# Edges of a four-stage graph network in two groups by source: rows of the last five blocks by one-hot products

## The chip, the core and the metric

The kernel runs on one core of one Trainium2 chip. The metric is the device time in microseconds of one execution; the smaller, the better. The engines are named as in the profile: PE (matrix products), PEld (PE's loads of the stationary operand, which overlap its products), DVE (VectorE), ACT (ScalarE), POOL (GpSimd) and SP (here only an issuer of DMAs).

## What is computed

There are 3125 nodes with 128 features and 53125 directed edges, sorted by destination, one of them a loop of each node. Four graph networks run one after the other, each followed by a residual sum and a layer normalisation:

```python
x = layernorm(x + gin(x))          # 4 layers: h = x + sum over edges of x[src]; x = relu(h@W1+b1)@W2+b2
x = layernorm(x + rgcn(x))         # relu(x@root + bias + sum_r mean_{edges of type r}(x[src]) @ W[r]), 8 types
x = layernorm(x + basis(x))        # relu(sum over edges of alpha[t]*x[src]@w_rel[t] + indegree * x@update), 16 types, 8 bases
x = layernorm(x + gated(x))        # relu(sum over edges of gate*(x[src]@W[r] + bias[r]) + x@loop), 8 types
# in gated: gate = sigmoid(dot(msg, gate_weight[r]) + gate_bias[r]), so it depends on the source node and r alone
# in basis: alpha = sigmoid(h@w2), h of the edge features, but taken by edge type (alphas[rels]): 16 rows count
```

## The kernel before

**The dense stage.** The four layers of the first network use one matrix, the number of edges from each source to each destination. It lies in SBUF as `AT`, bf16, 25 blocks of 128 sources by 3125 destinations. It is built from 416 tiles of 128 edges (the loop at L796 to L842): DVE makes two one-hot matrices of a tile, `ohs` of the source inside its block (L824) and `ohk` of source block and relative destination together (L826), PE multiplies them (L828, and L832 for the column shared with the tile before), and ACT writes the product to `AT` at a place held in a register (L835). Beside this loop, at the tiles listed in `LATE`, `late` turns the edges' keys (`turn`, four PE transposes and a copy each) into the layout with one edge per partition and stores them in DRAM as `keys` and `srcs`. The dense products of the first layer are woven into the loop (`under`). Then the layers run in seven chunks of up to 512 destinations each: `dense` multiplies 25 source blocks, each as three bf16 parts, with `AT` (75 products, L760), copies the sum out on DVE as `hT` (L765), applies the two weight matrices, and stores three bf16 parts of the result. The last layer's `norm` stores its rows to the DRAM table `fx0`.

**The relational stages.** The other three networks share `relational` (L1092). It goes over the 416 tiles in order of destination. For each tile POOL gathers the 128 source rows from a DRAM table (`gather`, L1062); DVE makes a one-hot matrix `oh` of 16 destinations by 8 relations (or bases), weighted in layers 2 and 3 (L1150, L1152, L1157); PE multiplies rows and one-hot in fp32 (L1159); and DVE adds the 128x128 product to `sums` at a column held in a register (L1161). `sums` holds, for each of the 128 features, node by relation. In layers 1 and 3 small products (L1167) count a tile's edges by destination and relation into one or two segments of 128 nodes; where they go comes from two registers per tile (`seg`, loaded on PE by `values`). Before a block of `sums` is used ACT clears it (L957).

When the last tile that can touch a block of 128 nodes is through, `finish` closes the block: eight products with the relations' weights (`by_relation`, L1183), the residual and the norm, and a store. In layer 1 the sums are first divided by the counts: `sel` products spread the reciprocal counts over all partitions (L1204), and DVE multiplies (L1205). The next layer gathers from the whole table that these stores make: `fx1` for layer 2, `gtab` (rows and eight gates) for layer 3. Between layers 1 and 2 sixteen edges' end rows are gathered (`f_xs`, `f_xd`) for the attention coefficients.

**What orders the work.** Each engine runs its own instructions in the order in which a scheduler placed them; engines wait for one another by semaphores. How far POOL's gathers may run ahead of PE is set by the pool `f_gat`: six buffers of four tiles. The product L1159 has three PSUM buffers.

Of the kernel before, what the change touches and what calls it, by code (L numbers as in the profile page):

```python
# [23 lines left out]
I32 = mybir.dt.int32  # L24
# [37 lines left out]
LATE = [16, 20, 24, 28, 32, 36]  # L62
# [452 lines left out]
def gin_layers(ctx: ExitStack, tc: tile.TileContext, a: dict, pre: dict, outer: ExitStack, eps, srcI, xtab):  # L515
# [13 lines left out]
    keys = dram.tile([P, 4, TE], F32, name="keys")  # L529
    srcs = dram.tile([P, TE], I32, name="srcs")  # L530

    AT = big.tile([P, NB, N + W], BF16, name="AT")
    places = keep_.tile([P, 2, TE], F32, name="places")
# [5 lines left out]
    lo, hi = pre["lo"], pre["hi"]  # L539
# [6 lines left out]
    for n, (name, pad) in enumerate((("dst", PADDST), ("src", 0), ("edge_type_8", 0), ("edge_type_16", 0))):  # L546
        eng = (nc.sync, nc.scalar)[n % 2]
        r = raw[name] = tmp.tile([QR, 4, P], I32, name="raw_" + name)
        nc.gpsimd.memset(r[96:QR], pad)
        e = a[name]  # L550
        flat = r.rearrange("q k p -> q (k p)")

        for q0, q1 in ((0, 96), (96, QR - 1)):
            eng.dma_start(flat[q0:q1, :], e[q0 * 4 * P:q1 * 4 * P].rearrange("(q p) -> q p", q=q1 - q0))
        eng.dma_start(flat[QR - 1:QR, :E - (QR - 1) * 4 * P], e[(QR - 1) * 4 * P:].rearrange("(q p) -> q p", q=1))
    early = keep_.tile([P, 1], F32, name="early")
    nc.scalar.copy(early, eps)
    make_identity(nc, ident)
    nc.gpsimd.iota(iotah, pattern=[[1, NK]], base=0, channel_multiplier=0, allow_small_or_imprecise_dtypes=True)
    nc.gpsimd.iota(iota, pattern=[[1, 2 * P]], base=0, channel_multiplier=0, allow_small_or_imprecise_dtypes=True)  # L560
# [11 lines left out]
    def fl(name, into=None):  # L572
        f[name] = into if into is not None else tmp.tile([QR, 4, P], F32, name="f_" + name)
# [14 lines left out]
    sbI = tmp.tile([QR, 4, P], I32, name="sbI")  # L588
    nc.vector.tensor_scalar(sbI, raw["src"], 7, None, op0=OP.arith_shift_right)
    sb = tmp.tile([QR, 4, P], F32, name="sb")  # L590
    nc.vector.tensor_copy(sb, sbI)
    kb = tmp.tile([QR, 4, P], F32, name="kb")
    nc.vector.scalar_tensor_tensor(kb, sb, float(WK), rel, op0=OP.mult, op1=OP.add)
    mod = tmp.tile([QR, 4, P], F32, name="mod")
# [17 lines left out]
    nc.scalar.copy(hi, dst0[:, 1, :])  # L612
# [11 lines left out]
    def later(i, r):  # L624
        t = tmp.tile([P, TE], F32, name="turned", bufs=2)
        turn(t, r, nc.scalar.copy)
        nc.sync.dma_start(keys[:, i, :], t)

    turnedI = tmp.tile([P, TE], I32, name="turnedI")

    def late(i):

        if i == 0:
            turn(turnedI, f["src"], nc.vector.tensor_copy)
            nc.sync.dma_start(srcs[:, :], turnedI)
        elif i == 1:
            later(0, rel)
        elif i == 2:
            t8 = fl("edge_type_8", sb)
            later(3, t8)  # L640
        elif i == 3:
            nc.vector.scalar_tensor_tensor(mod, rel, float(R8), f["edge_type_8"], op0=OP.mult, op1=OP.add)
            later(1, mod)
        elif i == 4:
            later(2, fl("edge_type_16", kb))
        elif i == 5:
            flat = f["dst"].rearrange("q k p -> q (k p)")
            inner = f["src"].rearrange("q k p -> q (k p)")[:, :4 * P - 1]
            nc.vector.tensor_tensor(inner, flat[:, :4 * P - 1], flat[:, 1:], OP.is_gt)
            nc.vector.tensor_reduce(found, inner, AX.X, OP.add)  # L650
            tmp_ctx.close()

    def checks(own):
# [25 lines left out]
        add(1, w[:, 0:1], float(N - W), OP.is_lt)  # L679
        rows = own.tile([1, 1], F32, name="rows")  # L680
# [122 lines left out]
    with tc.tile_pool(name="g_hot", bufs=4) as hots:  # L803
        old = None
        under = []
        for t in range(TE):
# [6 lines left out]
            if t == LATE[-1]:  # L813
# [5 lines left out]
                nc.scalar.dma_start(srcI, srcs[:, :])  # L819
                sp_pool = sp_ctx.enter_context(tc.tile_pool(name="g_parts", bufs=1, side="right"))  # L820
            if t % 4 == 1 and (t - LATE[-1]) // 4 - 1 in range(NCH):
                first_parts((t - LATE[-1]) // 4 - 1)
# [22 lines left out]
    keep_ctx.close()  # L845
    ep = outer.enter_context(tc.tile_pool(name="f_edges", bufs=1))
    edges = ep.tile([P, 4, TE], F32, name="edges")
    nc.scalar.dma_start(edges, keys[:, :, :])
# [38 lines left out]
    for j in range(NCH):  # L887
        run(dense(l, j, norm))
    sp_ctx.close()
# [16 lines left out]

def low(t):
# [10 lines left out]
def first_tile(c0):  # L918

    return min(t for t in range(TE) if low(t)[1] + W > c0)  # L920
# [3 lines left out]
def in_order(ctx: ExitStack, tc: tile.TileContext, a: dict, out: bass.AP, pre: dict):  # L924
# [7 lines left out]
    ident, iota, ones, lo = (pre[k] for k in ("ident", "iota", "ones", "lo"))  # L932
# [7 lines left out]
    srcI = own.tile([P, TE], I32, name="f_srcI")  # L940
    edges = gin_layers(tc, a, pre, ctx, eps, srcI, xtab[0])
    dlr, key8, et16, et8 = (edges[:, i, :] for i in range(4))

    big = ctx.enter_context(tc.tile_pool(name="f_sums", bufs=1, side="right"))
    gat = ctx.enter_context(tc.tile_pool(name="f_gat", bufs=6, side="right"))
    ohp = ctx.enter_context(tc.tile_pool(name="f_ohp", bufs=6, side="right"))
# [6 lines left out]
    zero = const.tile([P, 1], F32, name="f_zero")  # L953
    nc.vector.memset(zero, 0.0)

    def clear(b, engine=nc.scalar.copy):
        engine(sums[:, b * P * NR:(b + 1) * P * NR], zero.to_broadcast([P, P * NR]))  # L957

    clear(0, nc.vector.tensor_copy)


    offs = const.tile([1, TE], I32, name="f_offs")
    nc.vector.tensor_scalar(offs, lo, float(NR), None, op0=OP.mult)
    seg = const.tile([1, 2, TE], I32, name="f_seg")

    def segments(t):
        c = low(t)
        return range(c[0] // SEGN, min(NSEG - 1, (c[1] + W - 1) // SEGN) + 1)

    def spots(t, i):  # L970

        if len(segments(t)) <= i:
            return 0, SEGN + W
# [369 lines left out]
```

## Time and profile before

| | us |
|---|---|
| Runs of the kernel, median of 3 | 2834.49 |
| lowest and highest | 2826.18, 2836.43 |
| The profiled execution's own time | 2817.4 |
| its span in the trace | 2815.5 |

| Engine | busy us | share of the span |
|---|---|---|
| PE | 1940.1 | 69% |
| PEld | 1373.8 | 49% |
| DVE | 1164.4 | 41% |
| ACT | 497.1 | 18% |
| POOL | 1191.8 | 42% |

The mean granted clock of PE over the execution is 0.698 of full speed. A busy PE is not a PE at its peak[...]. Loads of registers, waits and DMA issues are not counted as busy. A line number in the profile is that of the listing above. A group of instructions is shown as line, engine, operation and operands (output, then inputs), with the number of instructions; an fp32 product appears as two records. What a wait is put down to is the event that came last: "issue" means that the engine waited for nothing the profile shows, and "remote" that the releaser is unknown to it.

### The profile page before, as it was taken

The numbers are of one execution on the slowest core, as the hardware profiler recorded it, in microseconds if no ns is written. First come the engines' busy times: TensorE is split into PE (matmuls) and PEld (weight loads), VectorE is DVE, ScalarE is ACT, GpSimd is POOL, SyncE is SP. The second block draws the span as 40 slices with busy tenths as digits, with TensorE's granted clock in tenths as the row PEclk, the third lists the DMA queues.
The fourth block names the chain that finished last, engine by engine and source line by source line (L and its number), as shares of the span: only waits on it lengthen the run. The fifth ranks groups of instructions, "written<-read, shape, count | busy, mean of one in ns | idle before, by whom it ended". The sixth has DMA issues, their size and how long they took to land.

```text
span 2815.5 us, 37365 instructions
## 1 busy us (share of the span) xinstructions
PE 1940.1 (69%) x10916; PEld 1373.8 (49%) x10916; DVE 1164.4 (41%) x4732; ACT 497.1 (18%) x1001; POOL 1191.8 (42%) x1263
## 2 busy tenths in 40 slices
PE   5798999998467777777545656665644666565666
PEld 2343444444355566566444545554433555454545
DVE  6777612123144444444433434443423343333443
ACT  5778511101200000000001222222220000000000
POOL 0000000000545555656546666666625555555552
PEclk9988899999555655656666666666665556566666
DMA  1000111021211111111111112111211222121121
GB/s 49 17 7 13 41 46 59 19 62 46 54 47 44 44 44 45 48 43 49 45 34 50 51 50 51 49 51 49 53 28 43 48 46 47 45 49 45 45 49 26
DMA packets 101232, 121.96 MB, mean 43 GB/s; under 512 B 25046, under 2 KB 80523, under 8 KB 101031
## 3 DMA queue, kind: packets, MB, share of 16 engines
q0 software_dynamic: 40000, 83.59, 12.3%
q1 hardware_dynamic: 50256, 28.48, 3.4%
q10 hardware_dynamic: 10774, 7.42, 0.9%
q8 instruction: 100, 1.64, 0.3%
q14 instruction: 102, 0.83, 0.1%
HBM read 104.55 MB, written 14.84 MB: 42 GB/s over the span
## 4 chain that ended last, share of the span: by engine, by line
PE 47%; another core or an unknown queue 17%; issue 15%; POOL 8%; DVE 7%; DMA 3%; ACT 2%; DVEq 0%; ACTq 0%; SPq 0%; POOLq 0%
PE acc L760 14%; PE pw L1159 12%; POOL xg L1062 8%; PE pm L1183 7%; PE pa L828 3%; PE pr L1204 3%; PE pc L1167 2%; DVE sums L1161 2%; PE pr L768 1%; PE pr L775 1%; ACT AT L835 1%; DMA xn<-in_x_dram 1%; PE pa L832 1%; DMA xg<-fx,f_srcI 1%
## 5 line engine op out<-in xcount | busy, mean ns | idle before, releaser
L1062 POOL DMA_INDIRECT xg<-fx,f_srcI x832 | 791.8, 952 | 1209.5 <-DMA f_gloop<-n_L_gnn_loop_weight_dram 703.8
L1159 PE MATMUL pw<-oh,xg 128*128 128x128 f32 x2496 | 669.2, 407 | 379.9 <-DVE sums L1161 155.0
L1159 PEld LDWEIGHTS pw<-oh,xg 128*128 128x128 f32 x2496 | 524.5, 283 | 471.1 <-DVE sums L1161 188.1
L1161 DVE TENSOR_TENSOR sums<-pw,sums 128x128 f32 x1248 | 358.6, 287 | 877.0 <-remote 428.6
L1062 POOL DMA_INDIRECT xg<-gtab,f_srcI x416 | 394.5, 948 | 341.4 <-PE pw L1159 171.3
L760 PE MATMUL acc<-AT,xs 128*128 128x512 bf16 (+1 forms) x2100 | 446.2, 357 | 1.1 <-DMA xs<-xsd 1.0
L760 PEld LDWEIGHTS <-xs 128*128 128x128 bf16 x2100 | 176.3, 100 | 197.0 <-issue 22.6
L835 ACT CAST AT<-pa 128x400 f32 x416 | 213.0, 512 | 65.5 <-PE pa L832 33.3
L828 PE MATMUL pa<-ohk,ohs 128*128 128x425 bf16 x416 | 170.2, 423 | 50.1 <-ACT AT L835 25.9
L826 DVE TENSOR_SCALAR ohk<-iotah,places 128x425 bf16<-128x425 f16 x416 | 139.1, 334 | 62.2 <-PE pa L832 56.2
L957 ACT COPY sums<-f_zero 128x1024 f32<-128x1024 f32 x74 | 75.2, 1042 | 378.2 <-PE pm L1183 160.7
L1152 DVE SCALAR_TENSOR_TENSOR oh<-f_dcol,edges,coef 128x128 f32<-128x128 f32 x416 | 137.0, 343 | 0.6 <-ACT coef L1109 0.6
L1157 DVE TENSOR_SCALAR oh<-p_iota,edges,g 128x128 f32<-128x128 f32 x416 | 135.5, 354 | 0.1
L1167 PE MATMUL pc<-hw,h 128*8 128x16 f32 x1456 | 85.3, 186 | 60.8 <-issue 56.1
L1150 DVE TENSOR_SCALAR oh<-p_iota,edges 128x128 f32<-128x128 f32 x416 | 119.1, 293 | 0.0
L1183 PE MATMUL pm<-f_gW,sums 128*128 128x128 f32 x400 | 100.5, 433 | 25.0 <-DVE sums L1161 18.6
L1204 PE MATMUL pr<-ci,f_sel 8*128 8x128 f32 x400 | 93.4, 379 | 31.5 <-DVE sc L1205 22.2
L1167 PE MATMUL pc<-hw,rg 128*8 128x16 f32 x1456 | 83.8, 182 | 39.9 <-issue 24.3
L1183 PEld LDWEIGHTS pm<-f_gW,sums 128*128 128x128 f32 x400 | 97.9, 336 | 26.3 <-DVE sums L1161 19.4
L1167 PEld LDWEIGHTS pc<-hw,h 128*8 128x8 f32 x1456 | 61.3, 90 | 98.4 <-issue 85.8
L1183 PE MATMUL pm<-f_bases,sums 128*128 128x128 f32 x400 | 100.9, 434 | 9.1 <-issue 7.8
L828 PEld LDWEIGHTS <-ohs 128*128 128x128 bf16 x416 | 42.5, 102 | 129.9 <-DVE ohk L826 85.7
(202 smaller groups left out, 1777.9 us busy)
## 6 DMA issues: line engine op xcount, KB each, us to landing
xg<-fx,f_srcI POOLq DMA_INDIRECT x832
xsd<-sp SPq DMA_DIRECT2D x18, 384.0 KB
xg<-gtab,f_srcI POOLq DMA_INDIRECT x416
xs<-xsd SPq DMA_DIRECT2D x9, 384.0 KB
xs<-xsd ACTq DMA_DIRECT2D x9, 384.0 KB
xb<-fx SPq DMA_DIRECT2D x49, 64.0 KB
gtab<-yg SPq DMA_DIRECT2D x25, 68.0 KB
fx<-y SPq DMA_DIRECT2D x25, 64.0 KB
```

The source lines that it names most:

```text
L760: nc.tensor.matmul(acc[:, :n], xs[s // BPB][:, s % BPB, i, :], AT[:, s, c0:c1], start=s == 0 and i == 0, stop=s == NB - 1 and i == 2)
L826: nc.vector.tensor_scalar(ohk, iotah, keyb[:, t:t + 1], None, op0=OP.is_equal)
L828: nc.tensor.matmul(ps, ohs, ohk, start=True, stop=t == 0)
L835: nc.scalar.copy(AT[:, :, bass.ds(og[t % GRP], W)], ps3[:, :, :W])
L1062: nc.gpsimd.indirect_dma_start(out=dst, out_offset=None, in_=table, in_offset=bass.IndirectOffsetOnAxis(ap=idx, axis=0))
L1152: nc.vector.scalar_tensor_tensor(oh.rearrange("p (d b) -> p d b", b=NR), W2["dcol"], dlr[:, u:u + 1], cgroups[u - u % GRP][:, u % GRP, :]. ...
L1157: nc.vector.tensor_scalar(oh, iota[:, :W * NR], key8[:, u:u + 1], gate, op0=OP.is_equal, op1=OP.mult)
L1159: nc.tensor.matmul(ps, x[:, u % 4, :D], oh, start=True, stop=True)
L1161: nc.vector.tensor_tensor(w, ps, w, OP.add)
L1167: nc.tensor.matmul(segs[j][:, bass.ds(spot[i][u], W)], r, hw[:, u % GRP, :], start=False, stop=u == last_tile(min(N, (j + 1) * P)))
L1183: nc.tensor.matmul(pb, s[:, r, :], w[:, r, :], start=False, stop=r == NR - 1)
L1204: nc.tensor.matmul(pr[:, r * P:(r + 1) * P], sel[:, h + r, :], ci, start=True, stop=True)
```

## The change

The edges are split into two groups by source. Group P holds those whose source is in the last five blocks of nodes (`KB = 5`, from node `S0 = 2560` on), in 80 tiles; group G the others, in 344 tiles. Inside a group the order by destination is kept.

- **Placing the edges.** `late` computes the rank of each edge in its group on 125 partitions of 425 edges (a scan and a product with a triangular matrix) and so its slot. `scatter` writes source, destination and types of 125 edges, 8 bytes each, to their slots in DRAM: 425 indirect DMAs on POOL, one with each tile of the build loop from the 30th on and the remaining 38 behind the loop. `arrange`, called after the third chunk of the last dense layer, reads the slots back and unpacks them on DVE, with two copies held where they stand in program order. The turning of four keys in `late` goes.
- **Rows of group P** are not gathered. The last five blocks of the table stay in SBUF as three bf16 parts (`parts`, made by `keep_parts` when such a block is finished). `fetch` takes a tile's source numbers, spread over all partitions by a DMA on SP (one for two tiles), compares them with five columns of node numbers on DVE, and multiplies: 15 bf16 products into `px`, copied out by ACT. `add_P` then makes a one-hot matrix of 62 destinations by 8 relations, one product of 496 columns into `pp`, adds the old first column group on DVE, and ACT overwrites the sums from there on; so nothing is cleared any more. `px` and `pp` have one PSUM buffer each.
- **Group G** goes as before through `gather`, from the first 2560 rows of the table alone, with five gather buffers instead of six and one PSUM tile of four parts. The calls of `fetch` and `add_P` are placed between its tiles (`upto`).
- **Counts:** one register per tile on PE (`loP`) and segments with a margin of 128, instead of two registers; layer 1 counts in bf16. For group P, whole windows are counted into `cntP`.
- **Layer 1's finish** multiplies first and divides afterwards: the counts are transposed, and eight operations on DVE each scale a relation's product and add it. The `sel` products, the bias product and L1205 go.
- The keys of the tiles (`regs`, `dlr`, `key8`) are worked out before layer 1 from the unpacked edges, on DVE, most of them on one row of 424 values.

The core of the diff:

```diff
+KB = 5
+S0 = (NB - KB) * P
+NTP = 80
+NTG = 344
+WP = 62
...
     def late(i):
...
+            nc.vector.tensor_tensor_scan(rank, flag2, none, 0.0, OP.add, OP.add)
...
+    def scatter(c):
+        st = nc.gpsimd.indirect_dma_start(
+            out=slots[:, :], out_offset=bass.IndirectOffsetOnAxis(ap=rowI[:, c:c + 1], axis=0),
+            in_=meta[:EP2, c, :], in_offset=None)
...
+            if t > LATE[-1]:
+                scatter(t - LATE[-1] - 1)
...
+    def arrange():
+        def last_in_line(x):
+            tc.keep_in_program_order(x)
+        held = meta[:, :NTT, :]
+        nc.gpsimd.dma_start(held.rearrange("p t f -> p (t f)"), slots.rearrange("(p t) f -> p (t f)", p=P))
+        last_in_line(nc.vector.tensor_copy(edges["dst"], held[:, :, 0]))
...
     for j in range(NCH):
         run(dense(l, j, norm))
+        if j == 2:
+            arrange()
...
-    gat = ctx.enter_context(tc.tile_pool(name="f_gat", bufs=6, side="right"))
-    ohp = ctx.enter_context(tc.tile_pool(name="f_ohp", bufs=6, side="right"))
+    gat = ctx.enter_context(tc.tile_pool(name="f_gat", bufs=5, side="right"))
+    ohp = ctx.enter_context(tc.tile_pool(name="f_ohp", bufs=4, side="right"))
...
+        def fetch(v):
+            if v % 2 == 0:
+                srcb = wk.tile([P, 2 * P], F16, name="srcb", bufs=4)
+                nc.sync.dma_start(srcb, flatrow[:, v * P:(v + 2) * P].to_broadcast([P, 2 * P]))
+                ohT = hot_src[0] = wk.tile([P, KB, 2 * P], BF16, name="ohTP")
+                for k in range(KB):
+                    nc.vector.tensor_scalar(ohT[:, k, :], srcb, colid[:, k:k + 1], None, op0=OP.is_equal)
+            if v % 4 == 0:
+                fetched[v // 4] = (wk.tile([P, 4, GX], F32, name="xP"),)
+            ohT, x = hot_src[0], fetched[v // 4][0]
+            px = psum.tile([P, GX], F32, name="px", bufs=1)
+            for k in range(KB):
+                for i in range(3):
+                    nc.tensor.matmul(px[:, :width_], ohT[:, k, v % 2 * P:(v % 2 + 1) * P], parts[layer][:, k, i, :width_],
+                                     start=k == 0 and i == 0, stop=k == KB - 1 and i == 2)
+            nc.scalar.copy(x[:, v % 4, :width_], px[:, :width_])
+
+        def add_P(v):
...
+            oh = onehot(v, gate)
+            ps = psum.tile([P, BANK], F32, name="pp", bufs=1)
+            nc.tensor.matmul(ps[:, :WP * NR], x[:, v % 4, :D], oh, start=True, stop=True)
+            if counted:
+                pq = psum.tile([P, P], F32, name="pm", bufs=2)[:R8, :WP]
+                nc.tensor.matmul(pq, r, g["hw"][:, q, :], start=True, stop=True)
+            if v > 0:
+                nc.vector.tensor_tensor(ps[:, :NR], ps[:, :NR], sums3[:, bass.ds(g["lo"][q], 1), :].rearrange("p d r -> p (d r)"), OP.add)
...
+            nc.scalar.copy(sums3[:, bass.ds(g["loA"][q], WP), :], ps[:, :WP * NR].rearrange("p (d r) -> p d r", r=NR))
...
+        for u in range(NTG):
...
+            gather(xg[:, u % 4, :width_], table, srcI[:, w:w + 1])
+            upto(last_of(range(NTP), min(N, low2(w)[1] + W)), True)
...
     def finish1(b, s, pc):
...
+        nc.tensor.transpose(pt[:, :R8], cntP[:, blk], ident[:R8, :R8])
...
             for r in range(BPB):
-                nc.tensor.matmul(pr[:, r * P:(r + 1) * P], sel[:, h + r, :], ci, start=True, stop=True)
-            nc.vector.tensor_tensor(sc[:, h:h + BPB, :], s[:, h:h + BPB, :], pr.rearrange("p (r d) -> p r d", d=P), OP.mult)
+                nc.tensor.matmul(pr[:, r * D:(r + 1) * D], s[:, h + r, :], rW[:, h + r, :], start=True, stop=True)
+            for r in range(BPB):
+                v = wk.tile([P, D], F32, name="acc")
+                nc.vector.scalar_tensor_tensor(v, pr[:, r * D:(r + 1) * D], ci[:, h + r:h + r + 1], acc, op0=OP.mult, op1=OP.add)
+                acc = v
...
-    relational(1, xtab[0][:N, :], D, finish1, beside1)
+    relational(1, xtab[0][:S0, :], D, finish1, beside1)
...
-    relational(2, xtab[1][:, :], D, finish2)
+    relational(2, xtab[1][:S0, :], D, finish2)
...
-    relational(3, gtab[:, :], GX, finish3)
+    relational(3, gtab[:S0, :], GX, finish3)
```

## The prediction

> **What bounds the kernel now.** I cut the span by stage first, because a mean over five unlike stages says little. The cuts come from the first instruction of each stage in the trace: the build of the adjacency starts at 97 us, the dense layers alone at 330, the relational layers 1, 2 and 3 at 708, 1434 and 2083. The columns are window, length, busy time of PE, PE's weight loads, VectorE (DVE), ScalarE (ACT) and GpSimd (POOL), then PE's granted clock, DMA share, GB/s.
>
> ```profile
> 97.00:330.00 233.00, 213.14 (x1108) 92.93 (x1107) 177.56 (x725) 181.26 (x355) 0.00 (x0) 0.85 0.03 10
> 330.00:708.00 378.00, 363.69 (x1953) 172.21 (x1951) 89.12 (x271) 47.90 (x77) 0.00 (x0) 0.98 0.17 51
> 708.00:1434.00 726.00, 500.43 (x3222) 408.27 (x3222) 309.53 (x1195) 57.55 (x115) 396.67 (x418) 0.60 0.17 44
> 1434.00:2083.00 649.00, 382.74 (x1603) 320.62 (x1603) 254.45 (x1063) 137.31 (x281) 396.88 (x417) 0.63 0.19 48
> 2083.00:2815.00 732.00, 428.49 (x2832) 359.55 (x2832) 273.86 (x1265) 20.54 (x76) 394.50 (x416) 0.62 0.20 45
> ```
>
> The two dense stages are PE's own (91 and 96% busy) and POOL does nothing in them. The three relational layers take 2107 us of 2815.5, and there no engine is full: PE 69, 59 and 59%, POOL 54 to 61%, and the clock is at 0.60 to 0.63. So I read next what the gathers wait for, and the start of a layer.
>
> ```profile
> L1062 POOL DMA_INDIRECT xg<-fx,f_srcI x832: 938/944/1626, 708.2 to 2041.0; - x167
> ...
>   PE pw L1159: 345.7, 104
>   issue: 329.7, 1068
> ```
> ```profile
> 708.17 1.10 POOL L1062 DMA_INDIRECT xg<-fx,f_srcI  x1 [703.75 <-DMA f_gloop<-n_L_gnn_loop_weight_dram]
> 709.58 0.94 POOL L1062 DMA_INDIRECT xg<-fx,f_srcI  x1 [0.31 <-issue]
> 710.83 0.94 POOL L1062 DMA_INDIRECT xg<-fx,f_srcI  x1 [0.30 <-issue]
> ```
> ```profile
> 708.00:735.00 27.00, 7.61 (x61) 5.40 (x62) 1.79 (x8) 5.42 (x6) 20.43 (x22) 0.50 0.23 60
> 1434.00:1462.00 28.00, 11.93 (x42) 8.19 (x42) 6.52 (x26) 1.73 (x7) 21.30 (x23) 0.50 0.19 49
> 2083.00:2110.00 27.00, 5.60 (x32) 4.41 (x32) 3.84 (x16) 0.17 (x2) 18.67 (x20) 0.50 0.23 52
> ```
>
> One gather is 0.94 us and 0.30 of issue, so 1.247 us apart: 416 of them are a floor of 519 us a layer, under 649 to 732. But 345.7 us of POOL's idleness end at the product L1159, which frees a buffer. So POOL is ahead of PE by its 24 buffers, and PE, with gaps, carries the rest. The last table shows where gaps are widest: at each layer's start POOL issues 20 to 23 gathers in a row and PE is busy only 5.6 to 11.9 us of 27.
>
> What fills the gaps elsewhere is read from the waits of the sums and from PE's queue:
>
> ```profile
>   remote: 428.6, 114
>   PE pw L1159: 317.6, 204
> ```
> ```profile
> L1056 PEldq TENSOR_LOAD <-f_seg x206: 329/591/1717, 700.4 to 2792.4; - x103
> L1056 DVEq TENSOR_LOAD <-f_offs x78: 1095/1098/1360, 702.8 to 2786.7; - x78
> ```
> ```profile
> 721.63 0.21 PE L1167 MATMUL pc<-hw,h 128*8 128x16 f32 x2 [1.32 <-issue]
> 723.76 0.18 PE L1167 MATMUL pc<-hw,h 128*8 128x16 f32 x1 [1.92 <-issue]
> 724.47 0.19 PE L1167 MATMUL pc<-hw,h 128*8 128x16 f32 x1 [0.53 <-issue]
> ```
>
> The first fence (idle before L1161, by what ended it): the trace names no owner for 428.6 us. The second: PE loads registers 206 times at 0.59 us. The third lies inside the first layer's start: small products stand 0.7 to 2.1 us apart and wait for nothing that is recorded, while POOL issues without a break. I have no cause for this; I use it only as a fact.
>
> **The change, part by part.** Sums are against the profiled run (2817.4 us, span 2815.5), which lies 17 us under the median of 2834.5.
>
> *Gathers.* 344 instead of 416 a layer: floor 344 x 1.247 = 429 us, 90 less. As POOL waits for PE, this is worth nothing by itself; it is worth what PE can use.
>
> *PE, removed.* 72 fewer products L1159 at 0.536 us (669.2 us over 1248 tiles): 39 us a layer. In layer 1 the `sel` products L1204 (93 us) and the bias products L1210 (18 us) go. Counting products fall from 728 to 596 a layer (85 us a layer before, 0.117 each), and layer 1 counts in bf16, where I take half: layer 1 saves 50, layer 3 15. Register loads fall from 103 to 43 a layer, 35 us in each of layers 1 and 3, which is queue time and not in the busy figures.
>
> *PE, added.* Fetch: 15 bf16 products of 128 columns for each of 80 tiles, 1200 a layer. No row has this shape. The nearest is the bf16 weight load of L760, also 128 columns (the groups by line: 176.3 us over 2100, 100 ns), and each fetch product needs one: 120 us. The Trainium skill, "TensorE: Matmul & The Clock Gate", section "Back-to-back issue gap", gives about 81 ns sustained for pairs of this width: 97 us, 23 less a layer, 69 in all. I keep the row; at the clock of 0.62 the same load would be 160 ns and 193 us. Wide products L1375: fp32, 496 columns, two records each as for L768 (128x512, 0.644 us a record): 1.29 x 80 = 103 us. So PE's work at these prices is: layer 1 500 - 39 - 111 - 50 + 223 + 10 (transposes of the counts) = 533; layer 2 383 - 39 + 223 = 567; layer 3 428 - 39 - 15 + 223 = 597.
>
> *The clock.* PE was granted 0.60 to 0.63 at 59 to 69% busy and 0.85 to 0.98 at 91 to 96% in the same trace. The added bf16 products are work that waits for no gather and stands singly between the gathered tiles, so PE should be fuller and faster. I take 50 to 55 us a layer off the old fp32 work (334 us in layer 2: 184 gathered, 100 L1183, 50 rest, by a sixth): 483, 512, 542. Without a gain in clock these 160 us are lost.
>
> *From work to time.* Before, PE filled 59 to 69%; the dense stages reach 91 to 96%. I take 80% between, since register loads, PSUM buffers of one (`px`, `pp`) and the unnamed gaps stay: 483/0.80 + 25 (43 loads at 0.59) = 629; 512/0.80 = 640; 542/0.80 + 25 = 703. Against 726, 649, 732: -97, -9, -29, together -135. The shorter layer starts are in this: gathers of a layer read only the first 20 blocks, so they start while the last five are finished. Only PE's idle time there can be saved, at 1400 to 1462 us 26 and at 2040 to 2110 us 35.
>
> *DVE and ACT* gain 80 wide one-hots, 200 compares and 80 adds on DVE and 160 copies on ACT a layer. A 128x512 fp32 operation is 0.69 us on DVE (L716) and L835's 128x400 0.51 us on ACT: +140 and +90 us less what goes (L1205, L957, 72 tiles at 0.6), so DVE near 375, 330 and 360 of 630 to 700. PE hides it; without that cover the chain product, add, copy of one P tile (about 2.2 us, one `pp`) would cost 80 x 2.2 = 176 us a layer. SP's 40 broadcasts of source rows have four buffers and stand among stores that are not waited for.
>
> *The new front.* Some 20 DVE operations of 125x425 at 0.58 us (12 us) replace four turns on PE and ACT beside the build. In the build DVE is 76% busy, so I take +5. Then 425 scatters, POOL's, from build tile 29 (115 us) at the gathers' 1.247: 530 us, done at 645. They are needed by `arrange`, held on DVE after the third chunk of the last layer; the next `hT` copy, queued behind it, was at 651.7. Reading the slots back and copying them (about 5 us) just fits: +5. Before layer 1, about 30 operations on one row of 424 (0.579 each for 1x416, L607) and the split of the last blocks stand on DVE between the last norm and the first sum, 712.8 before: 25 us, of which the 19 us of PE's idleness in the first 27 were lost anyway: +5, since gathers are there by then. I round these three to +10.
>
> Here a rule speaks against the change. By the rows, 137 gathers that ran under 0.6 us or more of a DVE one-hot lasted as long (median 944 ns) as the rest, so a scatter under the build should cost the same. The Trainium skill, "SBUF — State Buffer", section "SBUF: two separate sides", says that DVE in its fast two-port modes locks GpSimd out, so that a DMA's descriptors cannot be written. The build's one-hots are fast ones: (334 - 248)/(425 - 128) = 0.29 ns a column. If scatters moved only in DVE's free 24% until 330, about 41 of 172 would be done, 131 late by 163 us, and `arrange` would hold DVE, and then PE, some 150 us: 2840 rather than 2690. I take the row, with this as an upper bound. The lower bound is zero, since a wait cannot shorten the build.
>
> Sum: 2817.4 - 135 + 10 = 2692; against the median 2834.5 - 125 = 2710.
>
> **The rivals.**
>
> *PE becomes the bound and stays gappy* (0.22). For: 223 us of new work a layer, and the gaps without an owner are in PE's completions. Against: fill products without a DMA behind them. At the old 59 to 69%, say 70%: 715, 731, 799, together +138: 2835 + 148 = 2983. It decides from a filling of 74% down.
>
> *POOL's stream slows the dense layers* (0.22). Slower, one mechanism: POOL, silent under GIN before, now issues a DMA each 1.25 us from 115 to 645, the density at which PE got 28% (7.6 of 27) in the fence of the layer starts. For: that fence, three times. Against: there PE also waited for data, and a scatter moves 1 KB, a gather 64. Slowed by a fifth over 530 us: +106 and the gain is nearly gone; by 40%, +212, 2920. It decides from 24%. The late scatters above (+150) go with it.
>
> *Nothing moves* (0.06): both halves cancel within 14 us. That the split does nothing is excluded: 72 gathers a layer are gone from POOL's queue.
>
> **How the numbers follow.** My case has 0.50: 2710, from 2495 (filling 90%: layers 562, 569, 627) to 2815. About 0.5%, 14 us, is what can be told from no change here. Faster 0.50, same 0.06, slower 0.44. The range must reach into both slower cases: 2500 to 3040.
>
> **What would show it.** Layer lengths near 630, 640, 700 with PE near 80% and a clock over 0.7; gathers 344 a layer; no PE gap of 10 us or more at the layer boundaries. Wrong: dense chunks at more than 18.4 us under the scatters; a long wait of DVE at the unpacking, about 650 us; fetch products over 0.16 us; a clock still at 0.62; idle time at `px` or `pp`.

## The result: slower, and the profile after

The changed kernel takes 2989.93 us (median of 4; 2976.85 to 2999.73) beside 2831.64 for the kernel before: ratio 1.0557, 95% interval 1.0517 to 1.0596. The profiled execution's span is 2997.6 us. I forecast 2710.

First the stages, cut at 114 us inside the build, at the build's end, at the last dense chunk (835.9 us, 694.2 before) and at the end of each relational layer. Columns as in the tables before. (The build's first product stands at 22.0 us here and at 13.5 before; the 97 us that the prediction calls its start is about where the first dense products are woven in.)

```profile
114.00:453.00 339.00, 234.03 (x1039) 78.36 (x1050) 200.94 (x700) 175.34 (x343) 270.17 (x227) 0.82 0.11 8
453.00:836.50 383.50, 363.96 (x1897) 172.44 (x1930) 82.62 (x207) 34.86 (x61) 183.93 (x158) 0.98 0.20 44
836.50:1583.30 746.80, 566.79 (x3274) 408.25 (x3274) 393.23 (x1760) 96.34 (x307) 349.79 (x364) 0.70 0.18 45
1583.30:2262.60 679.30, 527.47 (x2882) 400.79 (x2882) 346.83 (x1338) 178.44 (x428) 333.81 (x346) 0.76 0.18 44
2262.60:2997.50 734.90, 573.57 (x3872) 421.43 (x3871) 349.37 (x1563) 96.39 (x293) 307.90 (x324) 0.76 0.18 39
```

All of the loss has two places. The last dense chunk ends 142 us later: the first chunk is 20 late (140.5 against 120.9), the build loses another 103 (its last tile at 451.7 against 328.6), and 19 come behind it, at the borders of the dense layers (their short last chunk takes 11.8 and 11.5 us in the first two, 4.5 and 4.6 before); each full chunk of the dense layers still takes 18.4 us. The relational part takes 2162 us instead of 2121, where I expected about 1990: PE has gaps of 22 to 24%, not far from the 20% I assumed, but more work in between.

What runs under the build, from the group tables for 120 to 440 us after, and 97 to 330 us before (POOL, ACT and DVE; the last columns are the idle time ahead and what ended it):

```profile
L705 POOL DMA_INDIRECT slots<-meta,rowI x214 | 255.1, 1192 | 65.2 <-issue 65.2
L899 ACT CAST AT<-pa 128x400 f32 x306 | 156.5, 511 | 153.3 <-PE pa L896 134.1 <-issue 5.5 <-remote 4.0
L890 DVE TENSOR_SCALAR ohk<-iotah,places 128x425 bf16<-128x425 f16 x305 | 112.9, 370 | 121.8 <-PE pa L896 110.7 <-issue 5.7 <-remote 1.6
L888 DVE TENSOR_SCALAR ohs<-iotah,places 128x128 bf16<-128x128 f16 x305 | 98.5, 323 | 0.0
```
```profile
L835 ACT CAST AT<-pa 128x400 f32 x340 | 174.0, 512 | 50.0 <-PE pa L832 29.5 <-ACT AT L835 1.0
L826 DVE TENSOR_SCALAR ohk<-iotah,places 128x425 bf16<-128x425 f16 x338 | 113.3, 335 | 50.5 <-PE pa L832 46.2
L824 DVE TENSOR_SCALAR ohs<-iotah,places 128x128 bf16<-128x128 f16 x337 | 83.5, 248 | 0.0
```

ACT's casts last as long as before, but wait 134 us for PE instead of 30. DVE's one-hots, beside the scatters, are 35 and 75 ns longer. A scatter is 1.18 us plus 0.30 of issue, 1.485 apart, not the gathers' 1.247.

In the relational layers the page's groups show this:

```profile
L1428 PE MATMUL pw<-oh,xg 128*128 128x128 f32 x2064 | 611.9, 389 | 262.5 <-DVE sums L1430 193.7
L1361 PE MATMUL px<-f_parts,ohTP 128*128 128x128 bf16 (+1 forms) x3600 | 374.9, 248 | 58.6 <-ACT xP L1363 39.7
L1375 PE MATMUL pp<-ohP,xP 128*128 128x496 f32 x480 | 304.9, 722 | 26.1 <-ACT sums L1384 20.4
```

The new products cost what was priced. But the product L1428 takes 611.9/1032 = 0.593 us a tile (0.536 before), and PE waits for the sum L1430. In the program as built, with its semaphores, 949 of the 1032 products wait for the sum of the tile just ahead; before, a product waited for the sum three tiles ahead. The changed kernel keeps them in one PSUM tile of four parts, and these parts are not four buffers.

### The profile page after: what moved, and what is told of

Read it like the earlier page. It is cut to its first block, busy times and chain, and to the rows that moved or that the text cites. A ratio compares the mean times of both kernels' runs of the same rounds, so it can differ in the third digit from the quotient of the medians.

```text
span 2997.6 us, 43204 instructions
## 1 busy us (share of the span) xinstructions
PE 2324.1 (78%) x13197; PEld 1501.7 (50%) x13247; DVE 1448.8 (48%) x5820; ACT 636.6 (21%) x1536; POOL 1505.9 (50%) x1478
## 3 DMA queue, kind: packets, MB, share of 16 engines
q0 software_dynamic: 46800, 70.50, 11.5%
## 4 chain that ended last, share of the span: by engine, by line
PE 61%; issue 13%; DVE 11%; POOL 5%; another core or an unknown queue 5%; DMA 3%; ACT 2%; DVEq 1%; SPq 0%; ACTq 0%; POOLq 0%
PE pw L1428 12%; PE acc L823 11%; PE px L1361 7%; PE pp L1375 7%; PE pm L1450 5%; POOL xg L1250 5%; PE pa L892 4%; PE pr L1475 3%; DVE sums L1430 3%; PE pa L896 2%; PE pc L1436 2%; DVE ohk L890 1%; PE pr L831 1%; PE pr L838 1%
## 5 line engine op out<-in xcount | busy, mean ns | idle before, releaser
L1250 POOL DMA_INDIRECT xg<-fx,e_src x688 | 663.1, 964 | 702.1 <-PE pw L1428 416.4
L1428 PE MATMUL pw<-oh,xg 128*128 128x128 f32 x2064 | 611.9, 389 | 262.5 <-DVE sums L1430 193.7
L1428 PEld LDWEIGHTS pw<-oh,xg 128*128 128x128 f32 x2064 | 429.8, 252 | 488.8 <-DVE sums L1430 304.3
L705 POOL DMA_INDIRECT slots<-meta,rowI x425 | 508.0, 1195 | 160.8 <-issue 129.2
L1430 DVE TENSOR_TENSOR sums<-pw,sums 128x128 f32 x1032 | 298.9, 290 | 507.2 <-PE pw L1428 228.6
L1250 POOL DMA_INDIRECT xg<-gtab,e_src x344 | 326.8, 950 | 414.5 <-PE pw L1428 246.2
L1361 PE MATMUL px<-f_parts,ohTP 128*128 128x128 bf16 (+1 forms) x3600 | 374.9, 248 | 58.6 <-ACT xP L1363 39.7
L1361 PEld LDWEIGHTS <-ohTP 128*128 128x128 bf16 x3600 | 297.4, 113 | 111.4 <-issue 92.5
L1375 PE MATMUL pp<-ohP,xP 128*128 128x496 f32 x480 | 304.9, 722 | 26.1 <-ACT sums L1384 20.4
L1450 PE MATMUL pm<-f_relw,sums 128*128 128x128 f32 x800 | 202.9, 428 | 11.1 <-DVE sums L1430 7.5
L1450 PEld LDWEIGHTS pm<-f_relw,sums 128*128 128x128 f32 x800 | 195.4, 334 | 26.5 <-DVE sums L1430 15.9
L1384 ACT COPY sums<-pp 128x496 f32 (+1 forms) x240 | 137.3, 572 | 306.9 <-DVE pp L1381 252.9
L1354 DVE TENSOR_SCALAR ohTP<-srcb,f_colid 128x256 bf16<-128x256 f16 x600 | 145.9, 289 | 35.4 <-PE px L1361 18.8
```

The lines of the kernel that those rows point to most:

```text
L705: st = nc.gpsimd.indirect_dma_start(out=slots[:, :], out_offset=bass.IndirectOffsetOnAxis(ap=rowI[:, c:c + 1], axis=0), in_=meta[:EP2, c, ...
L1250: nc.gpsimd.indirect_dma_start(out=dst, out_offset=None, in_=table, in_offset=bass.IndirectOffsetOnAxis(ap=idx, axis=0))
L1354: nc.vector.tensor_scalar(ohT[:, k, :], srcb, colid[:, k:k + 1], None, op0=OP.is_equal)
L1361: nc.tensor.matmul(px[:, :width_], ohT[:, k, v % 2 * P:(v % 2 + 1) * P], parts[layer][:, k, i, :width_], start=k == 0 and i == 0, stop=k = ...
L1375: nc.tensor.matmul(ps[:, :WP * NR], x[:, v % 4, :D], oh, start=True, stop=True)
L1428: nc.tensor.matmul(ps, xg[:, (x - NTP) % 4, :D], oh, start=True, stop=True)
```

## The experiments

**Two kinds of sets.** The kernel before was run anew beside each set of experiments. It took about 2830 us in two of these sets (as it had at first) and 2351 in the other three; both kinds were seen on the same chip. I call them long and short sets. What makes a set short is open: all three short ones, and no long one, had the kernel with late scatters among theirs. Ratios below stay inside a set.

**1. Scatters alone, long set.** `b_scat`: the kernel before with

```diff
+            if t > 28:
+                scatter(t - 29)
```

A scatter here writes 125 constant rows of 8 bytes to a table that nobody reads.

> The kernel before, with one thing added: 425 indirect scatters on POOL (125 rows of 8 bytes from a constant tile to a DRAM table that nobody reads), one with each build tile from the 30th on and the rest behind the loop; no new work on any other engine. Theory A (the indirect DMAs of POOL make the other engines learn late of each other's ends, so the build, which hands over between three engines four times a tile, is stretched): build ends near 440 us instead of 329, chunks of the dense layers stay at 18.4 us, relational layers as before, total 2920 to 2960. Rival B (the build was stretched by the new DVE work of placing the edges): build ends within 10 us of before, total 2830 to 2845. Rival C (POOL's stream slows PE itself): dense chunks become longer too, 20 us and more, total above 2990.

2909.88 against 2829.27 (1.0305; 1.0256 to 1.0354). The build ended at 384, not 440, the last chunk at 771.5 (+77), chunks stayed at 18.4 us. ACT's casts wait for PE as in the changed kernel:

```profile
L851 ACT CAST AT<-pa 128x400 f32 x340 | 174.2, 512 | 104.6 <-PE pa L848 86.4 <-ACT AT L851 5.0 <-issue 3.4
```

Theory A in kind; in size about half of the changed kernel's loss (49 of 103 us from the first chunk to the build's end, 77 of 142 up to the last dense chunk).

**2. POOL busy without a DMA.** `b_mem`: two memsets in the place of each scatter.

> The kernel before, with 425 pairs of POOL memsets (128x500 fp32, about 1.1 us a pair) in place of the scatters: POOL equally busy[...], but no DMA. Theory A (it is the DMA's issue): build ends within 15 us of before, total 2830 to 2850. Rival D (the shared port of VectorE and GpSimd: DVE's fast one-hots wait for POOL): DVE's one-hots are lengthened or start late, build ends 430 us or later, total 2920 and more, and ACT's idle time follows DVE's.

2863.36 (1.0137; 1.0100 to 1.0173). The group table of its build, 97 to 460 us:

```profile
L833 DVE TENSOR_SCALAR ohs<-iotah,places 128x128 bf16<-128x128 f16 x347 | 201.8, 581 | 0.0
L835 DVE TENSOR_SCALAR ohk<-iotah,places 128x425 bf16<-128x425 f16 x348 | 182.9, 526 | 6.4 <-PE pa L841 6.3
L844 ACT CAST AT<-pa 128x400 f32 x352 | 180.4, 513 | 70.9 <-PE pa L841 43.3 <-ACT xs L722 0.5
```

DVE's one-hots go from 248 and 335 to 581 and 526 ns. The Trainium skill, "SBUF — State Buffer", section "SBUF: two separate sides", says that VectorE in a two-port mode and GpSimd hold one shared pair of ports by an exclusive lock, each for a whole instruction. These lengths fit that; no run here shows in which mode the one-hots are. The waiting ate DVE's slack: the build ended 30 us later and the kernel took 34 longer, more than Theory A allowed and far less than rival D.

**3. Plain DMAs on POOL.** `b_plain`: `nc.gpsimd.dma_start` of the same bytes.

> The kernel before, with 425 plain POOL DMAs of the same 125 x 8 bytes (contiguous rows in DRAM) in place of the indirect ones. If any DMA that POOL writes descriptors for delays the others: build ends 400 us or later, total above 2890. If it is the index reading of the indirect form: build within 20 us of before, total 2830 to 2855.

2872.27 (1.0167; 1.0130 to 1.0204). Both expectations miss: the first chunk came 32 us late. The plain DMAs' issue begins at 4.5 us, at the kernel's start, and until 154 us ACT waits 40.6 us for the loads of `x` (18.8 before). From the first chunk on the build took 205 us, as before (208), with plain DMAs beside it until 282 us:

```profile
L845 ACT CAST AT<-pa 128x400 f32 x361 | 185.0, 512 | 51.1 <-PE pa L842 26.0 <-ACT AT L845 1.2 <-ACT xs L723 0.5
```

So a plain DMA delays the loads at the start, but not the handover from PE to ACT.

One number separates these runs, the lateness: how late ScalarE starts the cast after the end that the trace records for the product L896 (L832), or after its own last work if that was later. Worked out over the tiles after 100 us: 0.07 us on average before, 0.07 with plain DMAs, 0.08 with memsets, 0.23 with scatters, 0.43 in the changed kernel, in whose build a third or more of the tiles lie above 0.3. In the changed kernel that is 147 us in sum, against 23. The trace models the ends of products, so it can't tell a late message from a product that really ends later; that PE itself is not slowed is seen in the chunks of 75 products, still 18.4 us under the scatters.

**4. Scatters held behind the build.** `a_late`, run three times (`a_late2` and `a_late_three` are the same kernel):

```diff
-            if t > LATE[-1]:
-                scatter(t - LATE[-1] - 1)
...
+    nc.vector.tensor_scalar(z, AT[:EP2, NB - 1, N - 1:N], 0.0, None, op0=OP.mult)
+    nc.vector.tensor_tensor(rowI, rowI, z.to_broadcast([EP2, EC2]), OP.add)
+    for c in range(EC2):
         scatter(c)
```

> The changed kernel with all 425 scatters held behind the build: their row numbers take in a zero made from the last entry of the adjacency. Nothing else is moved. Theory A (the scatters stretch the build and nothing of the dense chunks): the build ends near 350 us instead of 452, chunks stay at 18.4 us under the scatters, which end 631 us after the build, near 980; the unpacking then holds VectorE and PE, the last chunk ends near 1025 instead of 836, relational layers as in the changed kernel, total 3150 to 3200. Rival E (half of the loss in the build is the changed kernel's own order of work or its new VectorE operations, since scatters added to the kernel before cost its build 55 us only): the build ends later than 380.

> The changed kernel with all scatters held behind the build, once more, where the kernel before takes its usual time (if this set shows 2830 again; the first such run stood in a set where it took 2351). Theory A: the whole loss in the build is the scatters': the build ends near 335 instead of 444 to 452, chunks of the dense layers stay at 18.4 us under the scatters, last chunk near 1030, relational layers as in the changed kernel (2140 us), total 3170 to 3200. Rival E (half of that loss is the changed kernel's own order of work): build ends later than 380.

> The changed kernel with all scatters held behind the build, in the same set. With 2351 before: 2880 as in both earlier runs. With 2830 before: build ends near 335 if the scatters are all that stretches it there, later than 380 if not; total 3170 to 3200.

2879.30, 2880.14 and 2883.21 against 2351, all in short sets. The build ended at 328 to 330, and the unpacking then held the next chunk back from 653 to 985. But in a short set the scatters cost the build only some 10 us anyway (experiment 8), so rival E, the changed kernel's own order of work, is refuted there alone. In a long set it was not tested.

**5. Scatters to the changed kernel's rows, short set.** `b_scat2`: row numbers spread as the change spreads them, and another source column each time.

> The kernel before with 425 scatters as before, but to the rows that the changed kernel would write (edges of one partition spread over the table by the low seven bits of their place) and from a different 8 bytes of each partition each time. The plain-addressed scatters cost the build 55 us (0.28 each in the build), the changed kernel's 0.49 each. If the addresses make the difference: build ends near 420 and total near 2960; if not: as with the plain addresses, build near 384, total 2905 to 2925.

2364.35 against 2350.62 (1.0054; 1.0036 to 1.0071), build end at 336. The question was about long sets; here neither address pattern costs much. `b_scat_three` repeated the plain addresses:

> The kernel before with 425 plain-addressed scatters under the build, in the same set. With 2351 before: build longer by under 10 us, total 2355 to 2370. With 2830 before: 2910 again, the ends of PE's products reaching ScalarE 0.23 us late on average instead of 0.07.

2363.34 against 2350.72 (1.0051; 1.0031 to 1.0071), lateness 0.07 us. In a short set the same indirect DMAs bring no lateness, and cost 13 us.

**6. One PSUM tile of four parts in the kernel before, long set.** `b_pw1`:

```diff
+    pw = psum.tile([P, 4, W * NR], F32, name="pw")
...
-                ps = psum.tile([P, W * NR], F32, name="pw", bufs=3)
+                ps = pw[:, u % 4, :]
```

> The kernel before with its products in one PSUM tile of four parts, as the changed kernel has it, and nothing else (1175 of 1248 products then wait for the sum of the tile just ahead, before it was three ahead). Theory H: a tile then takes 1.17 us or more of PE and VectorE in turn, beside counts and finishes (about 200 us a layer): layers of 620 to 700 on a chip where they took 524, total 2650 to 2850 against 2351; on a chip where they took 700, +100 to +200 in all. Rival (four parts are four buffers): no difference over 15 us.

3093.39 against 2830.18 (1.0943; 1.0908 to 1.0979): +263, even above the range. This edit alone costs more than the whole change does. The product itself grows with the wait for the sum ahead of it; first the kernel before, then this run:

```profile
L1159 PE MATMUL pw<-oh,xg 128*128 128x128 f32 x2496 | 669.2, 407 | 379.9 <-DVE sums L1161 155.0
```
```profile
L1160 PE MATMUL pw<-oh,xg 128*128 128x128 f32 x2496 | 930.2, 474 | 500.4 <-DVE sums L1162 383.5
```

That is 0.745 us a tile instead of 0.536, and the granted clock of the three layers is 0.51, 0.54 and 0.57, where it was 0.60 to 0.63.

**7. Group G alone, short set.** `a_noP`: `upto` does nothing, `sums` is cleared once.

> The changed kernel with all of group P's work in the relational layers left out (no fetch, no wide product, no copies, sums cleared once); the 344 tiles of group G and the finishes stay. It shows what group G costs alone. Theory F (0.6 us a gather beside PE's work, about 370 us of it): layers of about 575. If the gathers' own pace sets them: 430 to 480. Rival (a PE chain with gaps as before, 1.6 us a tile): 560 to 620 and P's work then costs 100 to 160 a layer, more than the 72 gathers that it replaces at 1.25 (90).

Layers of 618, 533 and 535 us: far above the 430 of the gathers' pace, though little is left beside the gathers. Its timeline inside layer 2:

```profile
1601.74 0.29 DVE L1432 TENSOR_TENSOR sums<-pw,sums 128x128 f32 x1 [0.63 <-PE pw L1430]
...
1602.08 0.79 PE L1430 MATMUL pw<-oh,xg 128*128 128x128 f32 x2 [0.38 <-DVE sums L1432]
1602.91 0.29 DVE L1432 TENSOR_TENSOR sums<-pw,sums 128x128 f32 x1 [0.56 <-PE pw L1430]
...
1603.25 0.80 PE L1430 MATMUL pw<-oh,xg 128*128 128x128 f32 x2 [0.38 <-DVE sums L1432]
```

Product (0.79), sum (0.29), product: they take turns, 1.17 us a tile, and the granted clock of this stage is 0.55.

**8. Two PSUM tiles for the changed kernel.** `a_pw2` (long set) and `a_pw2_three` (short set), with the changed kernel itself beside each, `after_again` and `after_three`:

```diff
-    pw = psum.tile([P, 4, W * NR], F32, name="pw")
...
-                ps = pw[:, (x - NTP) % 4, :]
+                ps = psum.tile([P, W * NR], F32, name="pw", bufs=2)
...
-        pt = psum.tile([P, P], F32, name="pm", bufs=2)
+        pt = psum.tile([P, P], F32, name="pm", bufs=1)
```

> The changed kernel itself, once more, beside the next two on one chip. The kernel before took 2829 us in the first set of experiments and 2351 in the second, on two chips; this run gives the changed kernel's time where the others of this set run. On a chip like the second (before about 2351: layers of 524 us, the gathers' own pace): build near 338, layers near 660, 560 and 620 as in the run with late scatters, total 2560 to 2600. On a chip like the first (before about 2830): 2990 as measured.

> The changed kernel with the product of group G back in PSUM tiles of its own, two of them in turn (the bank comes from the small products' pool pm, which goes from two to one). In the changed kernel 949 of 1032 such products wait for the sum of the tile just ahead; here for the one before that. Theory H (the one PSUM tile of four parts makes product and sum take turns, 1.17 us a tile in the run without group P): layers fall by 40 to 90 us each, total 120 to 250 under the changed kernel in this set. Rival (PE is full anyway, 78 to 87%): under 50 in total; or pm with one buffer costs as much as is won: within 30 or slower.

> The changed kernel itself, in a set that has the kernel with late scatters among its four, as both sets had in which the kernel before took 2351. If this set is such a one too: build 210 us from the first chunk on (not 311), last chunk near 735, layers 665, 560 and 622, total 2560 to 2600 beside 2351. If it is one like the others: 2980 beside 2830, and the kernel with late scatters, which then shows what its build takes there, has nothing to do with it.

> The changed kernel with two PSUM tiles for the products of group G, in the same set. In a set with 2351 before: the product and its sum no longer take turns, but PE's busy time (490 to 555 us a layer there) stays above the gathers' floor of 429: layers 600, 520 and 570, total 2430 to 2500, still above 2351. In a set with 2830: 2885 again.

| set | before | changed | with two tiles |
|---|---|---|---|
| long | 2830.18 | 2982.90 (1.0555) | 2885.32 (1.0191; 1.0152 to 1.0231) |
| short | 2350.72 | 2599.75 (1.1059) | 2308.15 (0.9819; 0.9790 to 0.9847) |

In the long set two tiles are worth 98 us, less than the 120 to 250 expected and more than the rival's "under 50". From the last dense chunk on the kernel takes 2062 us with two tiles and 2148 with one, PE is busy 1569 instead of 1654, and its granted clock by layer is 0.75, 0.81 and 0.79 instead of 0.69, 0.78 and 0.78. The product with two tiles:

```profile
L1427 PE MATMUL pw<-oh,xg 128*128 128x128 f32 x2064 | 500.0, 354 | 155.4 <-DVE sums L1429 66.1
```

That is 0.484 us a tile, where the changed kernel has 0.593 (0.592 in this set).

In the short set two tiles are worth 292 us. The kernel then beats the one before by 1.8%, where "still above 2351" was expected. What ended PE's idle time ahead of that product, first the changed kernel, then with two tiles (both short set):

```profile
  DVE sums L1430: 368.5, 759
```
```profile
  DVE sums L1429: 74.0, 179
```

And the three layers with two tiles, from its table of stages:

```profile
744.00:1295.00 551.00, 469.84 (x3276) 355.82 (x3277) 381.23 (x1754) 96.84 (x307) 357.11 (x364) 0.87 0.25 61
1295.00:1788.00 493.00, 427.07 (x2885) 340.68 (x2885) 333.08 (x1345) 176.61 (x427) 339.98 (x346) 0.95 0.25 61
1788.00:2308.00 520.00, 480.02 (x3870) 363.90 (x3869) 337.45 (x1562) 94.40 (x292) 313.69 (x324) 0.94 0.25 55
```

The clock is 0.87 to 0.95. The changed kernel's layers took 662, 554 and 630 in the same set, those of the kernel before (read in `b_scat_three`, whose layers are the same) 557, 554 and 548. In the short set the front still costs about 50 us, now for another reason, read in the changed kernel's waits of DVE, 600 to 730 us:

```profile
DVE e_dst L923 <- DMA meta<-slots: 35.9, 1, 35.9
```

The scatters end at 681 to 684 us in either kind of set; in the short set the dense layers are ready for the unpacking at 646, and wait. In the long set the dense layers come to it later, at 774. DVE's one-hots under the scatters are as long in the short set (395 and 295 ns on average) as in the long one (370 and 323), so their length is not what stretches the build.

**9. What PE's work and the gathers are worth in a short set.** `b_fill`: 15 products of constants at every fifth tile of the kernel before. `b_half`: `if layer == 3 or t % 2 == 0:` before its gather.

> The kernel before with 15 bf16 products of 128 columns added at every fifth tile of the relational layers (1260 a layer, as many as the changed kernel's fetch), on constant operands, read by nobody. About 100 us more of PE's work a layer and no new wait or gather. Theory G (PE's work counts, at a filling that stays near what it was): +120 to +150 a layer, total near 3220. Rival (PE's gaps take it in): 0 to +40 a layer, total under 2960; the granted clock rises above 0.65 in either case.

> The kernel before with every second gather left out in layers 1 and 2 (208 instead of 416; a tile without one uses the rows of the tile ahead); layer 3 is left as it is, as a control. The same work on PE, VectorE and ScalarE. Theory F (each gather costs the layer time by delaying what the engines hear of each other, 0.6 us or more each): layer 1 falls from 736 to 610 or less, layer 2 from 652 to 510 or less, the idle time of the sums put down to no owner mostly goes. Rival (PE's own work and its chain with VectorE set the layers, gathers are only ahead of them): both fall by less than 40.

1260 added products a layer cost 0.2% (2355.72 against 2350.58; 1.0014 to 1.0032), as the rival said: PE's gaps take them in. Half of the gathers left out (2104.53; it sums the wrong rows there): layer 1 about 65 us shorter, layer 2 181, layer 3 (the control) 547 as before. POOL's waits of `b_fill` inside layer 2 say why:

```profile
POOL xg L1064 <- issue: 88.7, 291, 0.3
```

It hardly waits for anything but its own issue. In a short set the kernel before runs at the gathers' pace, 416 x 1.25 = 520 us of 548 to 557. What each gather costs in a long set, which theory F asks, neither run can say.

**10. The two parts that need no groups.** `b_both` (long set): the finish of layer 1 and the counts from the change, in the kernel before. `b_pw4` (short set) adds a fourth product tile, at `pm`'s cost.

> The kernel before with only two parts of the change: layer 1 divides after the products (no sel products, no bias product, eight DVE operations per block), and counts with one register per tile and segments with a margin of 128, in bf16 in layer 1. No scatters, no groups. Theory (PE's work counts at about its busy time): layer 1 loses 93 + 18 + 40 us of PE and 35 of register loads, layer 3 35 of register loads: layer 1 near 620, layer 3 near 700, total 2690 to 2730. Rival (the pace of the gathers and the gaps without an owner set the layers; layer 2, which has neither counts nor sel, still takes 650): layer 1 falls to no less than 660, layer 3 by under 15, total 2740 to 2790.

> The kernel before with layer 1's division after the products, one register per tile's counts, and a fourth PSUM tile for the products of the gathered rows in exchange for one of the two of pm. With three tiles it took 2803 beside 2829. Theory H carried on (the number of product tiles is what lets PE go on while a sum is late; from one to three it was worth 263 us): another 20 to 60, total 2745 to 2785. Rival (three are enough, or the single pm tile costs it back at the finishes): 2795 to 2830.

`b_both`: 2803.24 against 2829.27 (0.9910; 0.9881 to 0.9938). Layer 1 lost 84 us of PE's busy time and 30 of its length; layer 2, untouched, was 14 longer and layer 3, with half the register loads, 9; so it gained less than even the rival allowed, and less work on PE is not less time. `b_pw4`: 2352.78 against 2350.62 (1.0009; 1.0002 to 1.0016): nothing to win at the gathers' pace. Its question, the fourth tile, was meant for a long set and stays open. So no version here beats the kernel before in both kinds of sets by measurement: `a_pw2` does in the short one (1.8%), `b_both` in the long one (0.9%); `b_both` as it is was not run in a short set.

## Why the prediction was wrong

The forecast for the profiled run was 2692 us, and it took 2999.5. Of these 307 us, 175 are the relational layers (+40 instead of -135) and 132 the front (+142 instead of +10).

- **"The clock"**: a sixth off the old fp32 work, 483, 512 and 542 us busy. Measured 567, 527 and 574. This is the step that failed: 131 us of work, at the measured filling (PE's busy share) of 76 to 78% about 170 of the 175. The granted clock did rise, to 0.70 to 0.76, but L1428 grew to 0.593 us a tile and L1450 stayed at 428 ns (L1183: 433). The cause that I did not see is in the diff that I described myself: the one PSUM tile of four parts. I named `px` and `pp` as single buffers and took `pw` for four. Experiments 6 and 8 show it in both directions inside long sets: the one tile alone takes the old product from 0.536 to 0.745 us, and two tiles in its place take it from 0.592 to 0.484, with 85 us less of PE's work. In the short set, with two tiles, PE is busy 470, 427 and 480 us, below my figures.
- **A size in the same sum**: the counting products were to save 50 and 15 us in layers 1 and 3. The lines L1436 and L1378 together saved 15 and nothing (85.3 to 69.9 us, 83.8 to 83.5), since I had left out the 80 products that count group P. These are up to 50 of the 131 us; two tiles gave back 85, which is about the rest.
- **"The front", +10**: measured +142. 103 of it lies in the build, 0.49 us for each scatter beside it. I priced scatters as gathers and asked only whether they would be late. Experiments 1 and 3 show that the indirect form, and not the plain one, delays the handovers from PE, 0.28 us for each scatter of `b_scat`. Why the changed kernel's cost more is open. That all of the 142 is the scatters' is argued, not shown: the lateness grows with it (0.43 us against 0.23), and in the short set, without lateness, the same new work of DVE costs 2 us up to the first chunk and 8 in the build; but in a long set the changed kernel was not run without scatters under its build. The pitch was wrong as well: at 1.485 us instead of 1.247 the scatters end at 681, not 645. In the long set the build's delay hid this; in the short set it costs the 36 us wait at the unpacking.
- **The first sum of layer 1** came 44.7 us after the last chunk, against 18.6: +26, where I had +5. It is part of the 175.
- **The rival "PE becomes the bound and stays gappy"** said 2983, and 2989.93 came. That is luck: it wanted a filling of 70% and +138 in the layers with the front at +10; measured were 76 to 78%, +40 and +142.
- **The rival "POOL's stream slows the dense layers"** had the engine, the sign and nearly the size (+106 to +212), but the wrong victim: chunks of 75 products without a handover did not slow at all; the build, which hands over at every tile, did.
- **The rule that spoke against the change**: I let the gathers' equal durations decide against the port lock. They could not: those gathers ran beside fp32 one-hots (293 to 354 ns for 128 columns), not the build's 16-bit ones. In the build the scatter keeps its length (1.172 us the shortest, 1.181 the median) and DVE's one-hots are longer (370 and 323 ns), but in the short set they are as long and the build loses only some 10 us.
- **Slips that decide nothing**: layer 2's old work is 383 - 39 = 344 us, not 334, and three terms of +5 make +15, not +10.
- **Right**: the prices of the fetch (374.9/3 = 125 us a layer against 120; 101 at a clock of 0.87 to 0.95) and of the wide products (102 against 103), and the filling near 80%. Of the signs of being wrong that I had named only idle time at `px` and `pp` showed, 59 and 26 us in all: chunks stayed at 18.4 us, DVE did not wait long at the unpacking, and the clock left 0.62. That fewer gathers alone bring little was not tested in a long set; in the short set of `b_half` they brought 65 and 181 us.

## What to carry to other kernels

A PSUM tile cut into parts is one buffer if products and reads of different parts wait for each other: count in the built program which earlier read each product waits for, before pricing anything else. Price a DMA moved under another stage by what that stage hands over, not by its bandwidth. Before a gap without an owner is built into a forecast, see whether the kernel shows it in every set of runs. A gain that rests on a higher clock needs a look at what makes PE stop between products.

## What the runs showed of the hardware

One kernel took 2830 or 2351 us by set, on the same chip, steadily within a set. The difference goes with lateness: an engine starts late after PE's recorded end while POOL issues indirect DMAs. Under the scatters it was 0.23 us a tile on average in `b_scat` and 0.43 in the changed kernel in long sets, 0.07 in short ones, with the DMAs themselves equally far apart (1.485 us in both). In the relational layers, beside the gathers, the same measure for DVE's sums after the product L1159 gives 0.38, 0.54 and 0.42 us a tile in the kernel before in a long set, 556 us in all, and 0.02 or less in `b_scat_three`, a short one with the same layers. That is enough for the 480 us between the sets. The 428.6 us that DVE's sums waited for no known owner before (the prediction's fence) are gone in that short run. In the build of the long sets plain DMAs and memsets on POOL did not cause it (0.07 and 0.08 us). What switches it on is not shown.
